# A two-layer graph attention, feed-forward and expert kernel: weight making moved to the first stage, rows written twice, rows in place

## The chip, the cores and the metric

The kernel runs on one core of a Trainium2 chip. The metric is the device time of one execution in microseconds. The engines are PE (matrix products), DVE (vector), ACT (scalar, with function tables), POOL (GpSimd) and SP (which issues most of the DMAs). A DMA that is issued on an engine's queue waits there for its semaphores in order with that engine's other work; it "lands" when its completion is signalled.

## The reference

All sizes: 4096 nodes, 256 features, 4 heads of 64 features, an int32 adjacency of 4096 x 4096.

```python
# --- layer 0 (adj_ffn) ---
x = x + _L0_gnn_ref(_layernorm(x, axis=-1), adj, L0_gnn_W, L0_gnn_a1, L0_gnn_a2)
x = x + _L0_ffn_ref((_layernorm(x, axis=-1))[None], L0_ffn_ln_w, L0_ffn_ln_b, L0_ffn_W, L0_ffn_b)[0]
# --- layer 1 (adj_ffn) ---
x = x + _L1_gnn_ref(L1_gnn_t, _layernorm(x, axis=-1), adj, L1_gnn_W1, L1_gnn_a1, L1_gnn_W2, L1_gnn_a2)
x = x + _L1_ffn_ref((_layernorm(x, axis=-1))[None], ...)[0]
```

The graph attention takes h = x W for each head, f1 = h a1, f2 = h a2, a softmax over the neighbours of leaky_relu(f1_i + f2_j), its product with h, and elu. The second layer has two of them. The feed-forward of layer 0 repeats this step 30 times:

```python
h = h + 0.01 * jnp.tanh(h)
h = h * jax.nn.sigmoid(h)
h = _layernorm(h, ln_w, ln_b)
h = jnp.einsum('bsc,dc->bsd', h, W) + b
```

The feed-forward of layer 1 is a mixture of 6 experts with the best 2 of each row.

## The kernel before

The program has five stages, one after the other: the first attention (g0), the feed-forward, the two attentions of layer 1 (g1, g2), and the experts. A group is 4 tiles of 128 rows (512 rows); there are 8 groups.

**Attention.** Each attention first prepares: it loads the 8 groups, normalizes, transposes and multiplies them (`products`, L300), and in g0 turns the adjacency into a bit mask, a piece at a time. During this preparation the functions in `others` make weights: `late.pop` (L418) runs them at g = 0 and after g = 3 and g = 5, with `small_ps` as their one buffer in PSUM. Then comes the loop over 4 chunks of 1024 rows, 4 heads and 8 units each, 128 units in all. A unit makes signs (`step_of`: ACT L461, DVE L459), masks them on DVE (L567 above, L573 below) and multiplies on PE (L519). At a head's end ACT takes the lower sums out of PSUM (L468, `lo`), DVE adds the whole sums into the tile `u` (L472), and `close` finishes the head, one step in each of the next units: L482 to L494 on DVE, the exponential into the tile `e` (L497), then `finish` of `to_rows` (L622, L623), which writes the head's 64 columns of 1024 rows with a DMA on SP (L624). In g0 `begin` also loads the old rows x (L615) that are added. Tile `u` has one buffer, `e` one of its own.

**Feed-forward.** `slot(at)` is a software pipeline of 240 units (30 steps x 8 groups) that are `at`, `at-2`, `at-3` and so on. In the order of the engines' work: tanh on ACT (L826) and its addition on POOL (L827) for unit `at`; silu (L815), the half-precision upper and lower parts (L817 on ACT, L818 on DVE) and a transposing DMA on SP (L822) for `at-2`; transposes on PE (L796), their copy on ACT (L846), the reciprocal deviation (ACT L849, POOL L850 and L851) for `at-3`; products on PE (L863, L866) for `at-4`; and for `at-5` the result on DVE (L803), scaled and with the bias added, into `y`. The last step adds `last` in place of `bias`, and then POOL adds the attention's rows (L877), which SP had loaded again from `x1d` (L790), and SP writes the sum to `x2d` (L878). g1 takes the groups 0 to 3 straight from these tiles and loads the others.

Ahead of the loop stands its preparation (L699 to L774): groups 0 to 3 of `x1d` are loaded on POOL's queue, `measure` (DVE L676, L678), `rate` (ACT L684, POOL) and `init` (ACT L695) normalize the rows into `y`, and the layer norm's weight and the matrix are loaded on ACT's queue (L703 to L707), transposed, scaled, centred, and split into `wT` and `w16`. The first slots measure, rate and init the other groups.

The order of PE, DVE, ACT and POOL within the loops is that of the program text (`tc.manual_schedule`). Outside them, and for SP, a scheduler orders the work; it keeps each engine's queue in order. Loads of whole groups go through `load_ahead` (L92) into tiles named `rows` of a pool that is made after g0; in g0 that place holds adjacency pieces (`adj`).

In the last stage `numbers` makes integer ramps on POOL (L959 iota, L961 cast).

Of the kernel before, what the change touches and what calls it, by code (L numbers as in the profile page):

```python
# [23 lines left out]
P = 128  # L24
C = 256
# [21 lines left out]
def gnn_ffn_kernel(ctx: ExitStack, tc: tile.TileContext, a: dict, out: bass.AP):  # L47
# [19 lines left out]
    ones = const.tile([2 * H, P], F32, name="ones")  # L67
    nc.gpsimd.memset(ones, 1.0)
# [10 lines left out]
    x1d = dram.tile([N, C], F32, name="x1d")  # L79
    x2d = dram.tile([N, C], F32, name="x2d")  # L80
# [7 lines left out]
    stream = []  # L88

    def load_ahead(src, g, view=rows_of, queue=nc.sync):  # L90
        t = stream[-1].tile([P, G, C], F32, name="rows")
        queue.dma_start(t, view(src, g))  # L92
        ahead[g] = t
# [67 lines left out]
    def attention(tag, src, norm, w, others, chunks, first, ends, following):  # L161
# [7 lines left out]
        with ExitStack() as scope:  # L169
            lay = scope.enter_context(tc.tile_pool(name=f"{tag}_lay", bufs=1))  # L170
            vals = lay.tile([P, NT, H, 2, 2, DV], F16, name="vals")
            r = lay.tile([P, NT, H], F32, name="r")
            nf2 = lay.tile([P, NT, H], F32, name="nf2")
            hs = lay.tile([P, 1, H, DV], F32, name="hs")
            mask = [scope.enter_context(tc.tile_pool(name=f"{tag}_mask", bufs=4))]
# [20 lines left out]
            def load_piece(n):  # L196

                c, g, part = n // PER, n % PER // 4, n % 4
                i0 = c * CM * P + part * TR
                arow[n] = stream[-1].tile([P, 2, 8 * P], I32, name="adj")  # L200
                nc.sync.dma_start(
                    arow[n],
                    adj[i0 : i0 + TR, g * 8 * P : (g + 1) * 8 * P].rearrange("(p s) n -> p s n", s=2),
                )
# [28 lines left out]
            with ExitStack() as ps:  # L233
# [44 lines left out]
                def greatest():  # L278
# [8 lines left out]
                    nc.vector.tensor_scalar(dm, ident[: 2 * H, : 2 * H], fx, None, op0=OP.mult)  # L287
                    pt = small_ps()
                    nc.tensor.matmul(pt[:, : 2 * H], ones, dm, start=True, stop=True)
# [108 lines left out]
                for g in range(NG + 2):  # L398
# [19 lines left out]
                    if g in (3, 5) and late:  # L418
                        late.pop(0)()
# [56 lines left out]
            def close(c, h, u):  # L476
# [19 lines left out]
                e = end.tile([P, CM, D], F32, name="e")  # L496
# [40 lines left out]
            with tc.manual_schedule(engines={mybir.EngineType.DVE, mybir.EngineType.Activation}):  # L537
# [3 lines left out]
                for at in range(len(units) + LAG):  # L541
# [43 lines left out]
                    if first:  # L585
# [8 lines left out]
                        if at == len(units) - 30:  # L594
                            store_mask(len(chunks) * PER // 4 - 1)
                    if following and at == len(units) - 2 * following[0]:
                        for g in range(following[0]):
                            load_ahead(following[1], g, *following[2:])
# [7 lines left out]
    def to_rows(dst, src=None):  # L606
# [5 lines left out]
        def begin(t, n, h, work):  # L612
            if src is not None:
                old = work.tile([P, 8, D], F32, name="old")
# [3 lines left out]
        def finish(t, n, h, u, e, old):  # L618
# [5 lines left out]
            nc.sync.dma_start(block(dst, t, n, h), e)  # L624

# [9 lines left out]
    with tc.tile_pool(name="adj", bufs=2) as adjacency:  # L635
        stream.append(adjacency)
        attention("g0", x, True, w0, [make, *makers], [8, 8, 8, 8], True, to_rows(x1d, x), [])
    stream.append(ctx.enter_context(tc.tile_pool(name="stream", bufs=4)))

    with ExitStack() as scope:
        one = scope.enter_context(tc.tile_pool(name="f_one", bufs=1))
        wT = one.tile([P, C], F32, name="wT")  # L650
        w16 = one.tile([P, 2, C], F16, name="w16")
        scale = one.tile([P, 2], F32, name="scale")
        under = one.tile([P, 2, G], F32, name="under")
        eps = one.tile([P, 2], F32, name="eps")
        nc.gpsimd.memset(eps[:, :1], EPS)
        nc.gpsimd.memset(eps[:, 1:], EPS * 1e-4)
        bias = one.tile([P, C], F32, name="bias")
        last = one.tile([P, C], F32, name="last")
# [4 lines left out]
        x1 = {}  # L663

        def load(g, queue=nc.sync):
            if g not in ahead:
                load_ahead(x1d, g, queue=queue)
            x1[g] = ahead.pop(g)

        measured, rates = {}, {}  # L670

        def measure(g):
            st = small.tile([P, G, 6], F32, name="x_st")
            mv = measured[g] = small.tile([P, G, 2], F32, name="x_mv")
            for r in range(G):
                nc.vector.bn_stats(st[:, r, :], x1[g][:, r, :])  # L676
            for r in range(G):
                nc.vector.bn_aggr(mv[:, r, :], st[:, r, :])  # L678

        def rate(g):  # L680

            mv = measured.pop(g)
            rs = small.tile([P, G], F32, name="x_rs")
            nc.scalar.activation(rs, mv[:, :, 1], AF.Identity, scale=1e-4, bias=eps[:, 1:])  # L684
            nc.gpsimd.tensor_tensor(rs, rs, mhalf, OP.pow)
            nm = small.tile([P, G], F32, name="x_nm")
            nc.gpsimd.tensor_tensor(nm, mv[:, :, 0], rs, OP.mult)
            nc.gpsimd.tensor_scalar(nm, nm, -1.0, None, op0=OP.mult)
            rates[g] = rs, nm

        def init(g):
            t = x1.pop(g)
            rs, nm = rates.pop(g)
            for r in range(G):
                nc.scalar.activation(  # L695
                    y[:, g * G + r, :], t[:, r, :], AF.Identity, scale=rs[:, r : r + 1], bias=nm[:, r : r + 1]
                )

        for g in range(4):  # L699
            load(g, nc.gpsimd)  # L700
        with tc.tile_pool(name="f_prep", bufs=1) as prep, tc.tile_pool(name="f_pps", bufs=1, space=PSUM) as pps:
            ln = prep.tile([2 * KC, P], F32, name="ln")
            nc.scalar.dma_start(ln[:KC], a["L0_ffn_ln_w"].rearrange("(k p) -> k p", p=P))  # L703
            nc.scalar.dma_start(ln[KC:], a["L0_ffn_ln_b"].rearrange("(k p) -> k p", p=P))
            wr = prep.tile([P, KC, C], F32, name="wr")
            nc.scalar.dma_start(wr, a["L0_ffn_W"].rearrange("(k p) c -> p k c", p=P))
            nc.scalar.dma_start(bias, bcast_rows(a["L0_ffn_b"]))  # L707
            for g in range(3):
                measure(g)
                if g < 2:  # L710
                    rate(g)
            init(0)
            ps = pps.tile([P, 2 * KC], F32, name="ps_ln")
            nc.tensor.transpose(ps, ln, ident[: 2 * KC, : 2 * KC])
            lnT = prep.tile([P, 2 * KC], F32, name="lnT")
            nc.vector.tensor_scalar(lnT, ps, 100.0, None, op0=OP.mult)
            lbb = prep.tile([P, KC, P], F32, name="lbb")
            nc.vector.tensor_copy(lbb, lnT[:, KC:, None].to_broadcast([P, KC, P]))
            ps = pps.tile([P, KC, C], F32, name="ps_w")
            for k in range(KC):  # L720
                for o in range(KC):
                    nc.tensor.transpose(ps[:, k, o * P : (o + 1) * P], wr[:, o, k * P : (k + 1) * P], ident)
            raw = prep.tile([P, KC, C], F32, name="raw")
            nc.vector.tensor_copy(raw, ps)
            ps = pps.tile([P, C], F32, name="ps_b")
            for k in range(KC):
                nc.tensor.matmul(ps, lbb[:, k, :], raw[:, k, :], start=(k == 0), stop=(k == KC - 1))
            nc.vector.scalar_tensor_tensor(bias, bias, 100.0, ps, op0=OP.mult, op1=OP.add)

            nc.vector.tensor_scalar(last, bias, -100.0, 0.01, op0=OP.add, op1=OP.mult)  # L730
            for k in range(KC):
                nc.vector.tensor_scalar(raw[:, k, :], raw[:, k, :], lnT[:, k : k + 1], None, op0=OP.mult)
            ps = pps.tile([P, C], F32, name="ps_m")
            for k in range(KC):
                nc.tensor.matmul(ps, mean, raw[:, k, :], start=(k == 0), stop=(k == KC - 1))
            for k in range(KC):
                nc.vector.tensor_tensor(raw[:, k, :], raw[:, k, :], ps, OP.subtract)
            sq = prep.tile([P, KC, C], F32, name="sq")
            nc.vector.tensor_tensor(sq, raw, raw, OP.mult)
            ps = pps.tile([P, C], F32, name="ps_m")  # L740
            for k in range(KC):
                nc.tensor.matmul(ps, mean, sq[:, k, :], start=(k == 0), stop=(k == KC - 1))
            far = prep.tile([P, 4], F32, name="far")
            nc.vector.tensor_reduce(far[:, 0:1], ps, axis=AX.X, op=OP.max)
            nc.vector.tensor_scalar(far[:, 0:1], far[:, 0:1], TINY, None, op0=OP.add)
            nc.gpsimd.tensor_tensor(far[:, 1:2], far[:, 0:1], mhalf[:, :1], OP.pow)
            nc.vector.tensor_tensor(far[:, 1:2], far[:, 1:2], far[:, 0:1], OP.mult)
            nc.vector.tensor_reduce(far[:, 2:3], bias, axis=AX.X, op=OP.max, apply_absolute_value=True)
# [33 lines left out]
        def slot(at):  # L782
            if 0 < at and at + 3 < NG:
                load(at + 3)
# [595 lines left out]
```

## Time and profile before

| | us |
|---|---|
| median of 3 runs | 3007.22 (3007.0 to 3009.08) |
| profiled execution | 3008.46 |
| its span | 3006.8 |
| g0, preparation | 0 to about 94 |
| g0, loop and closing | 94 to 606 |
| feed-forward | 606 to about 1581 |
| g1, loop | 1648 to 2126 |
| g2, loop | 2205 to 2677 |
| experts | 2677 to 3007 |

The page gives the busy time of the engines over the span, and the costliest groups of instructions with their mean duration, the idle time before them and what ended most of it:

```profile
PE 2813.1 (94%) x33923; PEld 2568.3 (85%) x33923; DVE 2741.0 (91%) x5766; ACT 2462.0 (82%) x3132; POOL 1173.2 (39%) x1056
L461 ACT ACTIVATE st<-f1b,nf 128x1024 int8<-128x1024 f32 x1265 | 1334.2, 1142 | 29.9 <-PE acc L519 24.6
L827 POOL TENSOR_TENSOR th<-th,y 128x1024 f32<-128x1024 f32 x240 | 568.2, 2368 | 27.2 <-ACT th L826 4.4
L803 DVE SCALAR_TENSOR_TENSOR y<-po,z_rs,bias 128x256 f32<-128x256 f32 x928 | 384.4, 477 | 2.1 <-PE tp L796 0.7
L815 ACT ACTIVATE z<-th 128x1024 f32<-128x1024 f32 x240 | 251.2, 1047 | 8.6 <-POOL th L827 8.3
```

Read the last of these lines so: 240 silus on ACT took 251.2 us together, 1047 ns each, and ACT stood idle 8.6 us ahead of them, 8.3 of it until POOL's addition was done. Lines of the timeline, shown below, give the start, the busy time, the engine, the line, the operation and how many are merged; in brackets stands the idle time before it and what ended it. "SPq" is a DMA issue on SP.

### The profile page before, as it was taken

Reading aid. Unit: us, or ns where it says so; the run is one execution under the profiler, and the core shown is the slowest. Engines: PE = TensorE matmul, PEld = TensorE weight load, DVE = VectorE, ACT = ScalarE, POOL = GpSimd, SP = SyncE. Lnnn points to the kernel's source line nnn. Section 1 sums busy time; section 2 is a strip of 40 time slices with the busy share of each in tenths; the row PEclk is TensorE's granted clock in tenths of the full one; section 3 lists DMA queues with packets and bytes.
Section 4 is the critical chain, followed back from the end, with each engine's and each line's share of the span. In section 5 each row is a group of like instructions: output and inputs, shape, how many; then the busy total and the mean of one; then the engine's idle time right before and its main releaser. Section 6 shows DMA issues by size and latency. Waiting matters only on the chain. (4 is left out here: it accounts for less than half of the span.)

```text
span 3006.8 us, 82646 instructions
## 1 busy us (share of the span) xinstructions
PE 2813.1 (94%) x33923; PEld 2568.3 (85%) x33923; DVE 2741.0 (91%) x5766; ACT 2462.0 (82%) x3132; POOL 1173.2 (39%) x1056
## 2 busy tenths in 40 slices
PE   6899999979999999999998999999889999986996
PEld 5799999958888888888876999999789999975996
DVE  8999999989999999999998899999689999986775
ACT  5799999788888888888866999999699999963442
POOL 2000000089999999999993000000200000013663
PEclk9999999989999999999999999999999999997998
DMA  9999784143333333333343031220303132133253
GB/s 292 267 256 249 224 247 118 33 133 70 68 68 67 68 70 69 68 68 68 68 95 121 20 103 51 76 79 27 107 20 93 51 107 79 51 96 123 82 172 134
DMA packets 482899, 320.08 MB, mean 106 GB/s; under 512 B 416573, under 2 KB 443354, under 8 KB 476378
## 3 DMA queue, kind: packets, MB, share of 16 engines
q1 hardware_dynamic: 467698, 287.13, 35.6%
q0 software_dynamic: 7680, 21.51, 2.3%
q10 hardware_dynamic: 7144, 6.16, 0.6%
q8 instruction: 268, 4.39, 0.6%
q14 instruction: 109, 0.89, 0.1%
HBM read 183.00 MB, written 52.04 MB: 78 GB/s over the span
## 5 line engine op out<-in xcount | busy, mean ns | idle before, releaser
L519 PE MATMUL acc<-vals,st 128*128 128x130 f16 x12288 | 1431.1, 218 | 36.1 <-DVE u L472 27.9
L519 PE MATMUL acc<-vals,below 128*128 128x130 f16 x12288 | 1430.7, 221 | 12.6 <-DVE below L573 11.9
L461 ACT ACTIVATE st<-f1b,nf 128x1024 int8<-128x1024 f32 x1265 | 1334.2, 1142 | 29.9 <-PE acc L519 24.6
L519 PEld LDWEIGHTS <-below 128*128 128x128 fp8e4 x12288 | 1175.7, 96 | 49.4 <-issue 44.5
L519 PEld LDWEIGHTS <-st 128*128 128x128 fp8e4 x12288 | 1207.5, 98 | 9.6 <-DVE st L567 7.5
L863 PE MATMUL po<-wT,zT 128*128 128x256 f32 x1920 | 576.1, 382 | 7.4 <-ACT zT L846 7.4
L827 POOL TENSOR_TENSOR th<-th,y 128x1024 f32<-128x1024 f32 x240 | 568.2, 2368 | 27.2 <-ACT th L826 4.4
L866 PE MATMUL po<-w,zT 128*128 128x256 f16 x3840 | 577.9, 273 | 0.3 <-DMA zT<-z 0.3
L866 PEld LDWEIGHTS <-zT 128*128 128x128 f16 x3840 | 376.3, 98 | 161.6 <-DMA zT<-z 1.2
L573 DVE TENSOR_TENSOR below<-m,st 128x1024 int32<-128x1024 int32 x384 | 470.0, 1224 | 32.8 <-DVE st L567 1.3
L567 DVE TENSOR_TENSOR st<-st,m 128x1024 int32<-128x1024 int32 x384 | 467.5, 1217 | 0.2
L803 DVE SCALAR_TENSOR_TENSOR y<-po,z_rs,bias 128x256 f32<-128x256 f32 x928 | 384.4, 477 | 2.1 <-PE tp L796 0.7
L839 DVE BATCH_NORM_STATS2 z_st<-z 128x6 f32<-128x256 f32 x960 | 335.8, 413 | 0.0
L863 PEld LDWEIGHTS po<-wT,zT 128*128 128x128 f32 x1920 | 291.1, 192 | 17.4 <-ACT zT L846 9.0
L105 POOL TENSOR_TENSOR ln_rstd<-ln_rstd,mhalf 128x4 f32<-128x4 f32 x24 | 32.3, 1345 | 586.5 <-ACT acc L1033 491.8
L815 ACT ACTIVATE z<-th 128x1024 f32<-128x1024 f32 x240 | 251.2, 1047 | 8.6 <-POOL th L827 8.3
L826 ACT ACTIVATE th<-y 128x1024 f32<-128x1024 f32 x240 | 249.8, 1041 | 0.1
L850 POOL TENSOR_TENSOR z_rs<-z_rs,mhalf 128x4 f32<-128x4 f32 x240 | 245.7, 1024 | 0.0
L846 ACT COPY zT<-tp 128x512 f32<-128x512 f32 x240 | 140.4, 585 | 110.5 <-PE tp L796 110.4
L459 DVE TENSOR_SCALAR st<-f1b,nf 128x1024 int8<-128x1024 f32 x271 | 201.2, 743 | 8.4 <-PE acc L519 8.4
L436 POOL MEMSET hs<- 128x4 f32 x3 | 0.3, 101 | 491.9 <-DVE u L489 491.9
L818 DVE SCALAR_TENSOR_TENSOR z<-z,scale,z 128x512 f16<-128x512 f32 x240 | 179.4, 747 | 4.9 <-ACT z L817 4.9
(252 smaller groups left out, 2970.2 us busy)
## 6 DMA issues: line engine op xcount, KB each, us to landing
adj<-in_adj_dram SPq DMA_DIRECT2D x64, 1024.0 KB
m<-edges SPq DMA_DIRECT2D x32, 1024.0 KB
f1b<-fd SPq DMA_DIRECT2D x48, 512.0 KB
edges<-m SPq DMA_DIRECT2D x16, 1024.0 KB
y<-yd SPq DMA_DIRECT2D x16, 512.0 KB
ew<-in_L_ffn_expert_w_dram SPq DMA_DIRECT2D x18, 256.0 KB
t<-in_x_dram SPq DMA_DIRECT2D x8, 512.0 KB
old<-in_x_dram SPq DMA_DIRECT2D x16, 256.0 KB
```

The source lines that it names most:

```text
L461: nc.scalar.activation(out, f1, AF.Sign, bias=f2, scale=-1.0)
L519: nc.tensor.matmul(acc[:, i, cols], masked[part][:, at_i // TR, s, rows], v[:, cols], start=(j == 0 and part == 0), stop=(j == NT - 1 and ...
L567: nc.vector.tensor_tensor(above, above, whole, OP.bitwise_and)
L573: nc.vector.tensor_tensor(below, whole, above, OP.bitwise_xor)
L803: nc.vector.scalar_tensor_tensor(y[:, g * G + r, :], po[:, r, :], rstd[:, r : r + 1], last if end else bias, op0=OP.mult, op1=OP.add,)
L815: nc.scalar.activation(z, th.pop(u), AF.Silu, scale=0.01)
L826: nc.scalar.activation(th[at], y[:, g * G : (g + 1) * G, :], AF.Tanh, scale=0.01)
L827: ins = nc.gpsimd.tensor_tensor(th[at], th[at], y[:, g * G : (g + 1) * G, :], OP.add)
L839: nc.vector.bn_stats(st[:, r, :], z[:, r, :])
L850: nc.gpsimd.tensor_tensor(rs[u], rs[u], mhalf, OP.pow)
L863: nc.tensor.matmul(po[:, r, :], src[:, r * P : (r + 1) * P], wT, start=True, stop=False)
L866: nc.tensor.matmul(po[:, r, :], src16[:, part * G + r, :], w16[:, other, :], start=False, stop=(part == 1 and other == 1),)
```

## The change

1. The feed-forward's weight making becomes `load_ffn` and `make_ffn`, a fourth entry of `others` in g0's preparation, run after g = 6. Some of its operations change engine: the copy out of PSUM, two scalings, the square and the upper half of `w16` go to ACT, `last`, a product and the two of `under` to POOL.
2. `to_rows` gets a `twin`: each head of g0 is written to `x1d` and once more to `x1e`.
3. In all three attentions `e` is no longer a tile: the exponential goes into the second half of `u`, and the DMA writes from there. `old` shares the buffers of `lo`.
4. `add_last` adds `last` to a group of `x1e` by an accumulating DMA on POOL's queue: groups 0 to 5 in g0's last chunk, groups 6 and 7 in the feed-forward's slots 32 and 64.
5. A table `side` calls into g0's last units: loads of the groups 0 to 3 at 28 units before the end, measures, rates, and the first two inits, which now work in place. Groups 4 to 7 go to a pool `hold`. In the first step tanh and the addition read these tiles, not `y`. After the first step each tile is loaded with its rows of `x1e`.
6. In the last step the result (L803 before) is added in place into that tile, and SP writes it to `x2d` at once; L877 and `last` as an operand are gone.
7. `ring`, one tile of 4 groups, takes the place of both pools, for the adjacency pieces and the rows; `ones` is gone (a factor C and `mean` instead); `numbers` makes long ramps in four parts.

The core of the diff (of `make_ffn` only what differs from L699 to L774 beside names):

```diff
-                e = end.tile([P, CM, D], F32, name="e")
+                e = u[:, :, 1, :D]
                 nc.scalar.activation(e[:, :nt], o[:, :nt], AF.Exp)
...
+                    if len(units) - at in side:
+                        side[len(units) - at]()
...
-                    if g in (3, 5) and late:
+                    if g in (3, 5, 6) and late:
                         late.pop(0)()
...
-                old = work.tile([P, 8, D], F32, name="old")
+                old = work.tile([P, 4, 2, DV], F32, name="old", tag="lo", bufs=2)
+                old = old.rearrange("p i b c -> p (i b c)")[:, : 8 * D].rearrange("p (i d) -> p i d", d=D)
                 nc.sync.dma_start(old[:, :n], block(src, t, n, h))
...
             nc.sync.dma_start(block(dst, t, n, h), e)
+            if twin is not None:
+                nc.sync.dma_start(block(twin, t, n, h), e)
...
+    def load_ffn(prep):
+        ln = w16[: 2 * KC, 0, :].bitcast(F32)
+        nc.scalar.dma_start(ln[:KC], a["L0_ffn_ln_w"].rearrange("(k p) -> k p", p=P))
+        nc.scalar.dma_start(ln[KC:], a["L0_ffn_ln_b"].rearrange("(k p) -> k p", p=P))
+        wr = wT, last
+        for k in range(KC):
+            nc.scalar.dma_start(wr[k], a["L0_ffn_W"][k * P : (k + 1) * P, :])
+        nc.scalar.dma_start(bias, bcast_rows(a["L0_ffn_b"]))
+        return ln, wr
...
+        nc.scalar.copy(raw, ps)
...
+        nc.gpsimd.tensor_scalar(last, bias, -100.0, 0.01, op0=OP.add, op1=OP.mult)
+        for k in range(KC):
+            nc.scalar.activation(raw[:, k, :], raw[:, k, :], AF.Copy, scale=lnT[:, k : k + 1])
...
+        nc.scalar.activation(sq, raw, AF.Square)
...
+        nc.gpsimd.tensor_tensor(far[:, 1:2], far[:, 1:2], far[:, 0:1], OP.mult)
...
+        nc.scalar.activation(w16[:, 0, :], raw[:, 1, :], AF.Copy, scale=scale[:, 1:])
...
+    def init(g):
+        rs, nm = rates.pop(g)
+        for r in range(G):
+            nc.scalar.activation(
+                x1[g][:, r, :], x1[g][:, r, :], AF.Identity, scale=rs[:, r : r + 1], bias=nm[:, r : r + 1]
+            )
+
+    def add_last(g):
+        nc.gpsimd.dma_start(rows_of(x1e, g), last[:, None, :].to_broadcast([P, G, C]), accum_op=OP.add)
...
+    side = {
+        28: [(load, g) for g in range(4)],
+        **{24 - 3 * g: [(add_last, g)] for g in range(6)},
+        14: [(measure, 0)],
+        8: [(measure, 1)],
+        4: [(rate, 0), (rate, 1), (measure, 2)],
+        1: [(measure, 3), (init, 0), (init, 1), (rate, 2), (rate, 3)],
+    }
+    attention(
+        "g0",
+        x,
+        True,
+        w0,
+        [make, *makers, (load_ffn, make_ffn)],
+        [8, 8, 8, 8],
+        True,
+        to_rows(x1d, x, x1e),
+        [],
+        {k: functools.partial(many, *v) for k, v in side.items()},
+    )
...
-            if 0 < at and at + 3 < NG:
-                load(at + 3)
             g = at - (units - NG - 4)
             if 0 <= g < NG // 2:
-                load(g)
+                load_ahead(x1e, g)
+                x1[g] = ahead.pop(g)
             elif NG // 2 <= g < NG:
-                x1[g] = work.tile([P, G, C], F32, name="x1", bufs=NG - NG // 2)
-                nc.sync.dma_start(x1[g], rows_of(x1d, g))
+                load_apart(x1e, g)
...
+                t = x1.pop(g) if end else None
                 for r in range(G):
                     nc.vector.scalar_tensor_tensor(
-                        y[:, g * G + r, :],
+                        t[:, r, :] if end else y[:, g * G + r, :],
                         po[:, r, :],
                         rstd[:, r : r + 1],
-                        last if end else bias,
+                        t[:, r, :] if end else bias,
                         op0=OP.mult,
                         op1=OP.add,
                     )
+                if end:
+                    nc.sync.dma_start(rows_of(x2d, g), t)
+                    if g < NG // 2:
+                        ahead[g] = t
...
-                nc.scalar.activation(th[at], y[:, g * G : (g + 1) * G, :], AF.Tanh, scale=0.01)
-                ins = nc.gpsimd.tensor_tensor(th[at], th[at], y[:, g * G : (g + 1) * G, :], OP.add)
+                was = x1.pop(at) if at < NG else y[:, g * G : (g + 1) * G, :]
+                nc.scalar.activation(th[at], was, AF.Tanh, scale=0.01)
+                ins = nc.gpsimd.tensor_tensor(th[at], th[at], was, OP.add)
...
-            if at + 2 < NG:
-                rate(at + 2)
-            if at + 1 < NG:
-                init(at + 1)
-            if at + 3 < NG:
-                measure(at + 3)
+            if 4 <= at + 3 < NG:
+                rate(at + 3)
+            if 2 <= at + 2 < NG:
+                init(at + 2)
+            if 4 <= at + 4 < NG:
+                measure(at + 4)
+            if at in (4 * NG, 8 * NG):
+                add_last(NG - 3 + at // (4 * NG))
...
-            u = at - 5
-            if units - NG <= u < units:
-                g = u % NG
-                t = x1.pop(g)
-                nc.gpsimd.tensor_tensor(t, t, y[:, g * G : (g + 1) * G, :], OP.add)
-                nc.sync.dma_start(rows_of(x2d, g), t)
-                if g < NG // 2:
-                    ahead[g] = t
```

## The prediction

> **What bounds the kernel now.** I read the page first (span 3006.8 us; PE busy 94%, DVE 91%, ACT 82%), then the busy time of each engine stage by stage, then the timeline around the feed-forward's two ends, then the timeline of the row writes. Columns of the first view: stretch, length, busy time of PE, weight loads, DVE, ACT, POOL, granted clock, DMA share, GB/s.
>
> ```profile
> 50.00:94.00 44.00, 29.29 (x126) 22.54 (x125) 41.91 (x77) 34.02 (x52) 15.98 (x24) 0.94 0.98 299
> 344.00:470.00 126.00, 119.78 (x2051) 118.28 (x2049) 122.64 (x130) 126.00 (x129) 0.00 (x0) 1.00 0.83 238
> 666.00:1545.00 879.00, 879.00 (x6280) 719.79 (x6279) 876.88 (x2915) 762.86 (x1122) 841.86 (x675) 1.00 0.35 68
> 1648.00:2120.00 472.00, 466.08 (x7996) 464.27 (x7997) 436.97 (x486) 437.05 (x441) 0.00 (x0) 0.99 0.18 57
> ```
>
> The second half of the first attention's preparation is bound by DVE (41.91 of 44.00). Its loop is bound by ACT (126.00 of 126.00) with DVE close behind. The feed-forward loop is bound by PE and DVE together; nothing in it is removed except at its ends. The second attention is PE's. So a gain can come only from the feed-forward's ends, and a loss from whatever lands on DVE or PE in the attentions.
>
> The start of the feed-forward, on DVE and ACT:
>
> ```profile
> 598.83 1.45 DVE L472 TENSOR_TENSOR u<-acc,lo 128x520 f32<-128x520 f32 x2
> ...
> 609.80 2.82 DVE L739 TENSOR_TENSOR sq<-raw 128x512 f32<-128x512 f32 x1
> 616.10 2.29 DVE L747 TENSOR_TENSOR far<-far 128x1 f32<-128x1 f32 x1 [0.70 <-POOL far L746]
> 621.74 0.72 DVE L818 SCALAR_TENSOR_TENSOR z<-z,scale,z 128x512 f16<-128x512 f32 x1
> 596.56 0.60 ACT L468 ACTIVATE lo<-acc 128x520 f32<-128x520 f32 x1 [8.64 <-PE acc L519]
> 620.44 0.72 ACT L817 ACTIVATE z<-z,scale 128x512 f16<-128x512 f32 x1 [1.86 <-DVE inv L763]
> ```
>
> The last head's closing starts at 598.83, and the weight's scale is ready only at 620.4, which ACT waits for. The end of the feed-forward:
>
> ```profile
> 1559.33 2.37 POOL L877 TENSOR_TENSOR rows<-rows,y 128x1024 f32<-128x1024 f32 x1
> 1561.65 2.80 POOL L827 TENSOR_TENSOR th<-th,y 128x1024 f32<-128x1024 f32 x1
> 1564.49 1.06 ACT L815 ACTIVATE z<-th 128x1024 f32<-128x1024 f32 x1 [4.44 <-POOL th L827]
> 1566.07 0.78 PE L863 MATMUL po<-wT,zT 128*128 128x256 f32 x2 [2.59 <-ACT zT L846]
> 1587.27 1.40 DVE L100 BATCH_NORM_STATS2 ln_st<-rows 128x6 f32<-128x256 f32 x4 [3.10 <-DMA rows<-x2d]
> ```
>
> The last additions (L877) stand on POOL ahead of the tanh additions (L827); ACT and then PE wait, and later DVE waits for a row load that stood on SP behind the writes of L877. Last, the row writes, which the change makes others wait for (SP and DVE):
>
> ```profile
> 1766.62 0.37 SPq L624 DMA_DIRECT2D h1d<-e  x1
> 1770.45 0.70 DVE L472 TENSOR_TENSOR u<-acc,lo 128x520 f32<-128x520 f32 x1 [0.74 <-ACT lo L468]
> 1796.62 0.37 SPq L624 DMA_DIRECT2D h1d<-e  x1
> 1799.22 0.92 SPq L92 DMA_DIRECT2D rows<-h1d  x2
> 1800.41 0.70 DVE L472 TENSOR_TENSOR u<-acc,lo 128x520 f32<-128x520 f32 x1
> PE acc L519 <- DVE u L472: 27.9, 45, 3.0
> ```
>
> A write issued at 1796.62 had landed by 1799.22, for then SP was let go to read it (2.6 us); the next use of u on DVE came 3.8 us after the issue. The last line (who waited for whom: total, times, longest) says that at nearly every head PE already waits for that DVE addition, so a delay there passes on to PE.
>
> **What the Trainium skill says.** "DMA: Bandwidth & Descriptors", section "Anatomy of one DMA — SWDGE (gpsimd) path", fits a DMA at about 2.0 us plus its bytes over 436 GB/s; for 256 KB that is 2.6 us, as the write at 1796.62 took, and for 512 KB 3.2 us, where the trace shows 6.0 us for POOL's row loads in the first attention, so I use the trace. The same page's "SWDGE vs HWDGE vs iDMA" gives accumulation during a transfer to GpSimd alone, so POOL issues the new ones; no such transfer is in the trace. Its "Rules for kernel authors" say that an accumulate beside another access of the same bytes must be waited for: hence the waits on SP below. "SBUF — State Buffer", "Who interferes with whom", says that a DVE instruction with two SBUF inputs contends with GpSimd's reads; L747, one element per partition, took 2.29 us beside 0.15 us for L750 of the same size, which agrees.
>
> **The change part by part.**
>
> *Weight making leaves the start.* Between 606.4 (last write issued) and 621.7 DVE has L728 to L772 in its way. In the changed kernel ACT's queue reads: both lower sums, tanh of 0, init 2, tanh of 1, the exponential of the last closing, init 3, table load, first z. The exponential needs DVE's closing chain, which starts no earlier than about 598.4 (measures 3, 4 and 5 at 1.75 each from 593.2) and takes 1.45 + 3 x 0.70 + 0.20 + 0.67 = 4.4 to it: 603. Then 0.63 + 2.06 + 1.28 + 1.05 + 0.72 puts the first low part of z16 (L818 before, L852 after) at about 610 instead of 621.74: 11.7 us. Slots with an init take 5.47 us (621.74 to 647.70 has five), those without 3.8; one init fewer stands in the slots, 1.7 more. Groups 6 and 7 still wait for the last row write (4.7 us from issue to landing at 606.39, now with a second write behind it) and may give a microsecond back. I take -13 (-10 to -14.5). Late next is ACT with its remaining inits.
>
> *That work in the first preparation.* DVE gets lnT 0.15, bias 0.42, two subtractions 0.75, two reductions 0.83, some nine small ones 1.3, wT 0.38 and w16 0.45: 4.3 us, where it is busy 41.91 of 44.00. PE's transposes and six products go through one small PSUM buffer, six more turns between PE and an evacuating engine; five more DMAs stand on ACT's queue ahead of its first computation at 15.43 (0.4 to 1.6 each for such issues there), with some 2.8 us until xT of the first group would be missed (the first weights are ready at 19.5). ACT and POOL have room. I take +5 (+2 to +10).
>
> *Rows written twice.* 16 more writes of 256 KB in 256-byte pieces, about 1.1 us of all 16 engines each (share 0.44 + 0.71 in the two microseconds of the write at 1797), per head of 31 us at a share of 0.83 to 0.91. Nothing in the first loop waits for DMA but 2.6 us once. Zero by itself; what it costs if the cover goes is the 4 heads of the first chunk times 1.1.
>
> *Rows in place: e becomes a part of u.* The additions into u (L472) now wait for the landing of the last head's writes; queued behind them on DVE are the mask operations, and PE waits for both. From write issue to next L472 the first loop has 3.5 to 5.95 us, seven of eleven intervals at 4.15 or more; the pair should land after 3.5 to 5. Stall 0 to 1 us on most, of which DVE's idle 0.8 us per head hides some: +5 (0 to +18). In the second and third attention (3.5 to 4.5 us for 2.6 to 3.2) there is room, except where 1 MB of mask is loaded just ahead: there DMA was busy until 1771.1, and L472 came at 1770.45. Six such heads, 0.5 to 1.5 with the chain behind: +3 (0 to +7).
>
> *Measures, init and rate at the end of the first loop.* Three measures (5.2 us) go into a chunk where DVE has 119.98 of 126.00 busy; inits fall into ACT's 8.64 idle. +1 (0 to +2).
>
> *Accumulating DMAs.* Six are in the first loop, with POOL idle. Two are in the feed-forward (slots 32 and 64): 0.75 to 1.2 us of issue on POOL, and on SP the load of that group stands ahead of a transposing DMA (L822) whose result PE takes about 2.3 us after it lands now. With 6.0 us to landing, much of it spent before that load's turn comes, this is just covered, with 10 it costs 4 each. Page and trace bound it at 3.2 and, doubled for reading and writing, 12. I take +1 (0 to +6).
>
> *The last step.* Eight L877 (2.35 each) go from POOL. Slots 238 and 239 took 6.3 us instead of 3.92: 4.8; PE's stop of 2.59 was followed by matmuls of 1.06 instead of 0.60 at a granted clock near 0.5, partly inside that. PE should end about 1574 instead of 1579.3: -5.3. The write no longer waits for POOL, so the load of group 4 goes out early and the 3.10 at 1587 goes: -2.7 more. DVE's own last row (PE to L803 to write) is late next. -8 (-5.5 to -9).
>
> *Integer ramps in four pieces.* In the last stage ln_rstd (L105) stands behind 4.3 instead of 6.7 us of POOL work, and DVE idled 2.4 there: -1.5 (-2 to 0).
>
> Sum: -13 -8 -1.5 +5 +5 +3 +1 +1 = -7.5. The profiled execution took 3008.46, its span 3006.8; the span after is then 2999.3, the execution about 3001. The median of the runs, 3007.22, is 1.2 below the profiled one, so 2999.7: **3000**.
>
> **Rivals.** (1) *The waits for landing decide* (the other side). Place: L472 at every head. 16 us of gain are left after the preparation and small costs of 7, so from a mean stall of 16 / 45 = 0.36 us per head the change doesn't pay. If the double write lands 2 us late in the first loop's heads (12 x 2 = 24) and the others lose 0.5 (33 x 0.5 = 16), it is 40 instead of 8: about 3032. For it: DMA share near 1 there and allowances of 3.5. Against: 2.6 measured in the quiet stages. (2) *Costs hidden*: preparation +2, waits +2, the gains whole at -22.5: 3007 - 18 = 2989. For it: DVE's spare time and PE's waits that are there already. (3) *The preparation eats the start*: one small buffer and late first ACT work cost 12 instead of 5: 3007. For it: DVE at 41.91 of 44; against: POOL and ACT are half idle. (4) The accumulates block SP: +6 more, inside the ranges.
>
> **How the numbers follow.** Forecast (2993 to 3006) 0.42; waits decide (3013 to 3045) 0.27; costs hidden (2984 to 2993) 0.18; preparation eats it (3001 to 3013) 0.13. A measurement of this kernel tells 0.2%, 6 us, from no change: below 3001.2 lie the hidden costs and most of the forecast (0.18 + 0.31), within lie the rest of it and the third rival (0.11 + 0.13), above lies the first. Range: 2986 to 3026, which leaves out a little below and about half of the first rival. The forecast's own is 2993 to 3006.
>
> **What would show it.** Right: the first L852 near 610 plus the preparation's and loop's delays; no idle above 1 us on ACT before the last tanh sums; the loop of the first attention beginning at 99 instead of 94. Wrong: DVE idle "<-DMA" at L472's successor above 10 us in sum, PE waits for it well above 27.9; idle on PE for zT in slots 32 and 64; the first attention's preparation longer by 10.

## The result, and the profile after

The changed kernel takes 3014.05 us (median of 18 runs, 3008.73 to 3017.73), the kernel before 3007.49 on the same chips; the ratio is 1.0021, 95% interval 1.0014 to 1.0028: 6 us slower, where 7 us faster was forecast. The profiled spans are 3013.7 and 3006.8.

The same DVE operations can be found in both traces (the addition into u, L472 before and L475 after; the lower part of z16, L818 and L852), and the difference of their start times is a lag that can be followed through the program:

| lag of the changed kernel at | us | step | forecast |
|---|---|---|---|
| first addition into u (g0's preparation and its first head) | 5.6 | +5.6 | +5 |
| first addition into u of g0's last head | 20.0 | +14.3 | +6 |
| feed-forward, slot 12 | 10.2 | -9.8 | -13 |
| feed-forward, slots 71 to 236 | 17.3 | +7.1 | +1 |
| first addition into u of g1 | 6.4 | -10.9 | -8 |
| last addition into u of g2 | 10.2 | +3.8 | +3 |
| end of the span | 6.9 | -3.3 | -1.5 |

All signs are as forecast. The gains are 24.0 us in sum (22.5 forecast); the losses are 30.8 instead of 15. The difference came mostly in the first loop and in the slots 32 and 64.

First, who waited for whom in the changed kernel (total us, times, longest). The first two lines are of the whole program, the third of g0's loop alone:

```profile
PE acc L522 <- DVE u L475: 37.3, 45, 3.2
DVE u L475 <- DMA h1d<-u: 11.3, 4, 5.5
DVE u L475 <- DMA x1e<-u: 6.9, 8, 1.8
```

The new waits for landing are there: with g2's, DVE's idle time for them is 22.2 us in 15 places. PE's wait for that addition went from 27.9 to 37.3. (The 5.5 in the second line is the closing of g1's last head, where DVE stood 4.5 us for ACT's lower sums before, too.)

The timeline of g0's fifth head and the one after it, on POOL, SP and DVE:

```profile
266.76 2.93 POOL L766 DMA_DIRECT2D x1e<-last  x2 [167.48 <-DMA x1e<-u]
271.03 6.40 SPq L220 DMA_TRANSPOSE m<-pair  x1
288.49 1.23 DVE L217 TENSOR_SCALAR pair<-ring 128x2048 int8<-128x2048 int32 x1 [2.62 <-DMA ring<-in_adj_dram]
301.91 0.70 DVE L475 TENSOR_TENSOR u<-acc,lo 128x520 f32<-128x520 f32 x1 [1.68 <-DMA x1e<-u]
```

Two accumulating DMAs start at 266.8, two more at 397.4, and only the last two in the last chunk, at 524.1: POOL has nothing else to do in this loop, and its queue waits only for a chunk's writes to land. DMA is full at 266.8. A transposing DMA of the mask then takes 6.40 us to issue (at most 2.97 in g0's loop before), and DVE stands for an adjacency piece and for a landing. This head is 4.5 us longer. The slow issue alone does not explain it: behind the pair at 397.4 a transposing DMA takes 7.07 us, but DVE doesn't stand for a piece there, and that head is 0.2 longer.

Slot 32 of the feed-forward, on POOL, SP and PE:

```profile
759.81 1.37 POOL L766 DMA_DIRECT2D x1e<-last  x1
767.57 1.47 POOL L885 TENSOR_TENSOR z_rs<-z_rs,mhalf 128x4 f32<-128x4 f32 x1
782.76 1.02 POOL L885 TENSOR_TENSOR z_rs<-z_rs,mhalf 128x4 f32<-128x4 f32 x1
766.79 0.36 SPq L802 DMA_DIRECT2D x<-x1e  x1
772.97 0.61 PE L903 MATMUL po<-w,zT 128*128 128x256 f16 x4 [3.09 <-DMA zT<-z]
774.42 1.06 PE L900 MATMUL po<-wT,zT 128*128 128x256 f32 x2
```

The accumulating DMA is issued at 759.8; SP's load of that group, which waits for it, goes at 766.8, so it took 7.0 us to land. The transposes behind it on SP come late, PE stands 3.09 us, and then its matmuls take 1.06 instead of 0.60 for some 3 us. The lag grows by 4.9 here. At slot 64 the same wait is 1.88 us, the matmuls keep their 0.60, and the lag grows by 2.0. Remember POOL's power (the operation that makes the reciprocal deviation, L850 before, L885 after), with 1.47 just behind slot 32 and 1.02 once PE had stood: it matters below.

The feed-forward's start, on DVE:

```profile
620.09 2.55 DVE L485 TENSOR_TENSOR u<-u,r 128x520 f32<-128x520 f32 x1
622.68 2.85 DVE L489 TENSOR_TENSOR u<-u 128x520 f32<-128x520 f32 x1
633.03 0.75 DVE L852 SCALAR_TENSOR_TENSOR z<-z,scale,z 128x512 f16<-128x512 f32 x1 [3.66 <-ACT z L851]
```

The weight making is gone, but two additions of the closing take 2.55 and 2.85 instead of 0.70. At the other end the DVE line that waited 3.10 us for its rows now waits 0.57:

```profile
1595.87 1.41 DVE L101 BATCH_NORM_STATS2 ln_st<-ring 128x6 f32<-128x256 f32 x4 [0.57 <-DMA ring<-x2d]
```

### The profile page after: what moved, and what is told of

The parts are those of the page before. It is cut to its first block, busy times and chain, and to the rows that moved or that the text cites. A ratio compares the mean times of both kernels' runs of the same rounds, so it can differ in the third digit from the quotient of the medians.

```text
span 3013.7 us, 82658 instructions
## 1 busy us (share of the span) xinstructions
PE 2807.6 (93%) x33923; PEld 2568.8 (85%) x33923; DVE 2736.0 (91%) x5756; ACT 2465.6 (82%) x3137; POOL 1168.4 (39%) x1061
## 5 line engine op out<-in xcount | busy, mean ns | idle before, releaser
L522 PE MATMUL acc<-vals,st 128*128 128x130 f16 x12288 | 1437.5, 219 | 48.9 <-DVE u L475 37.3
L862 POOL TENSOR_TENSOR th<-th,y 128x1024 f32<-128x1024 f32 x232 | 549.9, 2370 | 23.6 <-DVE z L852 4.4
L900 PEld LDWEIGHTS po<-wT,zT 128*128 128x128 f32 x1920 | 291.1, 192 | 11.7 <-ACT zT L881 3.4
L885 POOL TENSOR_TENSOR z_rs<-z_rs,mhalf 128x4 f32<-128x4 f32 x240 | 248.7, 1036 | 3.1 <-ACT z_rs L884 3.1
L861 ACT ACTIVATE th<-y 128x1024 f32<-128x1024 f32 x232 | 241.7, 1042 | 0.0
L852 DVE SCALAR_TENSOR_TENSOR z<-z,scale,z 128x512 f16<-128x512 f32 x240 | 179.9, 750 | 8.2 <-ACT z L851 8.1
```

The costliest lines, as they stand in the source:

```text
L522: nc.tensor.matmul(acc[:, i, cols], masked[part][:, at_i // TR, s, rows], v[:, cols], start=(j == 0 and part == 0), stop=(j == NT - 1 and ...
L861: nc.scalar.activation(th[at], was, AF.Tanh, scale=0.01)
L862: ins = nc.gpsimd.tensor_tensor(th[at], th[at], was, OP.add)
L885: nc.gpsimd.tensor_tensor(rs[u], rs[u], mhalf, OP.pow)
L900: nc.tensor.matmul(po[:, r, :], src[:, r * P : (r + 1) * P], wT, start=True, stop=False)
```

## The experiments

Every ratio is to the kernel before on the same chip, with a 95% interval. "Loop" is the growth of the lag from the first to the last head of g0 (additions into u, first of each head), 14.3 in the changed kernel.

**The exponential in u alone.** The kernel before, with `e = u[:, :, 1, :D]`.

> The kernel before with one edit: the exponential goes into the second half of u and the row write starts there; one write for each head, nothing else. Theory A (the waits of the additions into u for the landing of a row write cost what the traces show): g1 and g2 lose 3 to 4 us at the heads with a mask load just ahead, g0 loses 2 to 4, together +5 to +8 us. Rival B (those stalls only move a wait that PE had anyway): under 2 us.

Measured: 1.0041 (1.0027 to 1.0055), 12 us slower, nearly twice what was expected in the middle. In the trace g0's additions waited 6.1 us for landings (9 times), its loop is 5.5 longer, and g1 and g2 lost 4.7. So theory A is right in kind, and its numbers were too small; one small edit that frees a tile costs about half of the 24.0 us that the whole change gains.

**Two writes alone.** The kernel before, with the second DMA in `finish`.

```diff
             nc.sync.dma_start(block(dst, t, n, h), e)
+            if twin is not None:
+                nc.sync.dma_start(block(twin, t, n, h), e)
```

> The kernel before with each head of g0 written twice from the tile e, which nothing reads afterwards; no wait is added for DVE. If the bytes alone cost the first loop its time (DMA share near 1), the loop of g0 gets 4 to 10 us longer and the transposing DMAs of the mask take longer to issue on SP; if only the wait for the second landing costs, it is within 1 us of before.

Measured: 1.0006 (0.9997 to 1.0015), loop +1.9, of which 0.3 in the first three chunks, where the mask is made and DMA is full. The bytes alone cost nothing that can be told from zero.

**The early accumulations held back.** The changed kernel; in `add_last`, for g < 6 (shortened):

```diff
+            tc.add_manual_dep(ins.ins, masked_last[0].ins.name, ..., reason="not before this unit")
```

> The changed kernel with the six accumulating DMAs of g0 held back to the units of the last chunk by a dependency on a mask operation there. Theory: in the changed kernel they start as soon as a chunk's writes have landed, two at 266.8 us, where the DMA engines are full, and cost the head after it 3 to 4 us: the time falls by 3 to 5 us. Rival: their transfers fit in, and the long head is that of the double writes: within 1 us of the changed kernel.

Measured: 1.0013 (1.0003 to 1.0023) where the changed kernel has 1.0021: 2 us, less than expected and with intervals that overlap. In the trace the head in question is 0.7 longer instead of 4.5, the next one 1.7 instead of 0.6, and the loop is 11.7. In the other runs that issue them at the same point this head is 2.0 to 4.5 longer when the additions into u wait for landing, and 0.7 when they don't (the run without waits, below): the accumulations cost mostly through these waits.

**SP freed in the slots 32 and 64.** The changed kernel; the loads of groups 6 and 7 depend on a late operation of the loop:

```diff
-                load_apart(x1e, g)
+                load_apart(x1e, g, lowers[-1] if g >= 6 else None)
```

> The changed kernel with the loads of the groups 6 and 7 of x1e held back to the feed-forward's last step, so that SP does not wait for the accumulating DMAs of the slots 32 and 64 ahead of the loop's transposing DMAs. Theory (SP is blocked): the lag of 4.9 and 2.0 us at these slots goes, -6 to -7 us, and no PE idle for zT is left there. Rival (the issue on POOL and its port cost them): -1 us or less.

Measured: 1.0072 (1.0056 to 1.0089), 21 us slower than before. Both numbers failed. As the theory said, PE doesn't stand for `zT` in these slots any more, and the lag at slot 36 is smaller (7.4); but from there it grows by 0.1 us in every slot, 22 us to the loop's end. The rival named the issue on POOL, which the next two runs bear out, but expected no gain and no loss. Who waited for whom, and POOL's and DVE's timeline in the middle of the feed-forward:

```profile
ACT z L857 <- POOL th L871: 127.6, 209, 1.9
1206.06 2.36 POOL L871 TENSOR_TENSOR th<-th,y 128x1024 f32<-128x1024 f32 x1
1208.39 1.46 POOL L894 TENSOR_TENSOR z_rs<-z_rs,mhalf 128x4 f32<-128x4 f32 x1
1209.93 0.20 POOL L895 TENSOR_TENSOR z_rs<-z_rs,under 128x4 f32<-128x4 f32 x1
1208.01 0.96 DVE L860 SCALAR_TENSOR_TENSOR z<-z,scale,z 128x512 f16<-128x512 f32 x1
```

The same three in the kernel before, in a slot of 3.92 us:

```profile
1002.73 1.02 POOL L850 TENSOR_TENSOR z_rs<-z_rs,mhalf 128x4 f32<-128x4 f32 x1
1003.83 0.42 POOL L851 TENSOR_TENSOR z_rs<-z_rs,under 128x4 f32<-128x4 f32 x1
1003.44 0.74 DVE L818 SCALAR_TENSOR_TENSOR z<-z,scale,z 128x512 f16<-128x512 f32 x1
```

POOL's three operations follow each other without a gap: 2.36 + 1.46 + 0.20 = 4.02 us per slot, where PE's slot is 3.92 and POOL had 2.36 + 1.02 + 0.42 = 3.80 before. In the kernel before, the power runs mostly beside the results that DVE reads out of PSUM (L803), and the multiplication behind it beside DVE's lower part; now the power starts beside the lower part (0.96 instead of 0.74). That this is what makes it longer is read from what stands beside it in nearly all slots of both kinds; no run separates it. ACT waits for POOL in nearly every slot. In the changed kernel, while PE stood and DVE with it, POOL caught up and then stood itself (3.56 us for DVE at 780.4), and the power went back to 1.02. The block of SP cost 7 us there and, by the 22 of this run, saved some 15 (an estimate from these two runs).

**A bump on POOL, without any DMA.** The kernel before; in slot 32 only:

```diff
+                if at == 4 * NG:
+                    nc.gpsimd.tensor_tensor(junk, y[:, :2, :], y[:, 2:4, :], OP.add)
```

> The kernel before with one more addition on POOL in the feed-forward's slot 32 (128 x 512, about 1.2 us; nothing reads its result) and no other edit, no DMA. Theory (the feed-forward's loop has two steady states, and a delay on POOL of over a microsecond takes it from 3.92 us per slot to about 4.02, where POOL's square root stands beside a DVE operation on the shared port and takes 1.47 instead of 1.02): from slot 35 on the lag grows by about 0.1 us per slot to the end, +15 to +21 us in all. Rival (the loop catches up with such a delay, and the slow state needs a DMA or a late load): +2 us or less.

```profile
751.13 1.27 POOL L854 TENSOR_TENSOR junk<-y 128x512 f32<-128x512 f32 x1
754.68 1.46 POOL L851 TENSOR_TENSOR z_rs<-z_rs,mhalf 128x4 f32<-128x4 f32 x1
```

Measured: 1.0067 (1.0048 to 1.0086), 20 us slower for one operation of 1.27 us. The lag is 1.7 at slot 30, 4.7 at slot 62 and 22.8 at slot 235. As expected, then: the loop of the kernel before has two steady states, and once it is in the slower one, where POOL has no gap, it doesn't leave it in the 200 slots that follow. The profile before had the sign already: in the loop's last step, where L877 delays POOL, two powers took 1.46 (the first at 1557.6).

**No accumulation in the loop.** The changed kernel; groups 6 and 7 loaded late, and POOL adds the constant:

```diff
-            if at in (4 * NG, 8 * NG):
-                add_last(NG - 3 + at // (4 * NG))
+            if units <= at < units + 2:
+                t = x1[at - units + 6]
+                nc.gpsimd.tensor_tensor(t, t, last[:, None, :].to_broadcast([P, G, C]), OP.add)
```

> The changed kernel without accumulating DMAs in the feed-forward's loop: the groups 6 and 7 are loaded late and POOL adds the constant after the loop. Theory (the issue on POOL puts its square root beside a DVE operation that uses the same port, a state of 4.02 us per slot that stays until PE stops; the block of SP ended it in the changed kernel): no lag at the slots 32 and 64, all slots at 3.92, the time falls by 7 us. Rival (the late loads of groups 6 and 7 bring the slow state themselves, since they were in the run free_sp too): slots at 4.02 again, 10 us or more slower than the changed kernel.

Measured: 1.0006 (0.9997 to 1.0014), 4 to 5 us below the changed kernel's 1.0021. The lag stays at 10.0 from slot 30 to slot 235, so all 7.1 us of the loop are gone, and late loads are harmless. (The scheduler put the two additions into the last slots, where the lag grows by 3 us.)

**The waits for landing taken away.** The changed kernel, both writes kept:

```diff
-                e = u[:, :, 1, :D]
+                e = u[:, :, 1, :D] if first else end.tile([P, CM, D], F32, name="e")
...
-            nc.vector.scalar_tensor_tensor(e, e, 1.0, u, op0=OP.min, op1=OP.add)
+            out = e if old is None or dst is x3d else old
+            nc.vector.scalar_tensor_tensor(out, e, 1.0, u, op0=OP.min, op1=OP.add)
+            e = out
```

In g0 the tile `old` takes its turn with `lo`, so ACT's second lower sum may wait for a landing, later than the addition did. (The expectation names g2 beside g0; in the kernel that ran, g2 writes from the exponential's own tile, as g1 does.)

> The changed kernel with the waits for landing moved away from the additions into u, both writes kept: in g0 and g2 the last operation of a head puts its result into the tile old, from where it is written, and in g1 the exponential has a tile of its own. Theory A (those waits are most of the 14.3 us that the first loop lost and all that g1 and g2 lost): the loop of g0 gets 6 to 9 us shorter than in the changed kernel, g1 and g2 together 3 to 4, the time falls by 8 to 12. Rival (the bytes of the second write and the accumulations cost the loop its time): g0 keeps its loss, and the time falls by 3 to 4.

Measured: 1.0002 (0.9994 to 1.0011), 5 to 6 us below the changed kernel. The loop is 8.7 instead of 14.3; from g1's first to g2's last addition the lag grows by 1.0 instead of 3.8. Theory A holds in kind, with 5.6 and 2.8 where it said 6 to 9 and 3 to 4. Of the 5.6, 3.7 are in the one head beside the accumulating DMAs.

**The weights loaded later.** The changed kernel; the five DMAs of `load_ffn` depend on a later copy of `xT`.

> The changed kernel with the five DMAs of the feed-forward's weights on ACT's queue held back until a third group's transposes are copied. Theory (they delay ACT's first copy, which came at 22.2 us instead of 16.7, and the preparation never wins that back): the first addition into u comes 4 to 5 us earlier and the time falls by as much. Rival (DVE's added 4.3 us in its full half are the cause): 1 us or less.

Measured: 1.0027 (1.0017 to 1.0037). ACT's first copy came at 16.9 us, as before the change (16.7), and not at 22.2; the first addition into u still came 5.5 late. So ACT's late copy is not what makes that addition late. Whether it is DVE's 4.3 us or the turns through one PSUM buffer wasn't separated.

**The closing not disturbed.** The changed kernel; POOL's additions of slots 0 and 1 depend on the closing's multiplication (L497).

> The changed kernel with POOL's first two additions of the feed-forward held behind the multiplication that ends the last head's closing. Theory (these additions, which now stand beside the closing, stretch its two additions on DVE from 0.70 to 2.55 and 2.85 us, and so the exponential and the first silu come 4 us late): the two take 0.70 again and the feed-forward's slot 12 comes 3 to 4 us earlier after the end of g0. Rival (what the closing gains, the later additions lose again): 1 us or less.

The operation that took 2.55, and who waited longest on DVE in the first slots:

```profile
619.32 0.70 DVE L486 TENSOR_TENSOR u<-u,r 128x520 f32<-128x520 f32 x1
DVE x_st L746 <- DMA x<-x1d: 6.8, 1, 6.8
```

Measured: 1.0026 (1.0016 to 1.0037). The closing takes 0.70 for each again, and slot 2 comes 10.2 after the last head's first addition into u instead of 14.2. But the measure of group 6 stands behind it on DVE and waits 6.8 us for the group's load, which waits for the last row write; slot 7 comes 1.3 later than in the changed kernel. So the rival holds for the time, and the theory for the two long additions.

**All of it together, three times.** One write to `x1d`, to which the constant is accumulated for groups 0 to 3 in the last chunk, after they are loaded; POOL adds it for groups 4 to 7; no wait at the additions into u; weights loaded later.

> All of it together, and no second copy: the rows are written once to x1d, the constant is accumulated there for the groups 0 to 3 after they have been loaded, in the last chunk, and POOL adds it for the groups 4 to 7 after the loop; no wait for landing at the additions into u; weights loaded after the first groups. From the traces: 6.9 us over before, less 4 (loads), less 8 to 12 (waits), less 7 (loop), less 1 to 2 (bytes): 13 to 18 us faster than before, near 2992.

Measured: 1.0076 (1.0063 to 1.009). The scheduler put POOL's four additions into the slots up to 10. The lag grows by 8.5 us from slot 5 to slot 10, and the loop stays in its slower steady state for the 230 slots that follow. g0's loop is 5.8, g1 and g2 lose nothing.

> The run best with two dependencies more: POOL's additions of the constant stand behind the loop's last addition, so that nothing disturbs POOL in the loop, and the first two additions of the feed-forward stand behind the closing. Expected from the other runs: the preparation +3 to +6, the loop of g0 +6, the start of the feed-forward -13, no lag in the loop, its end -10, g1 and g2 0, the experts 0 to -3: 11 to 16 us faster than before, about 2994.

Measured: 0.9967 (0.9955 to 0.9979), 10 us faster than before; this chip took 3024.12 for the kernel before. The loop of the feed-forward keeps its lag (4.1 from slot 30 to 235).

> The run best2 with the measures, rates and inits of the groups 6 and 7 one slot later. In best2 DVE stood 5.9 us at the measure of group 6 for that group's load, which waits for the last row write. Theory (that wait holds up the lower part of the next slot, so it is what is late next after the closing): slot 3 comes 4 to 5 us earlier and the time is 3 to 5 us below best2, about 0.9955 of before. Rival (the init that now stands a slot later costs as much): the same as best2, 0.9967.

Measured: 0.9963 (0.995 to 0.9977), 2996.64 where the kernel before takes 3006.87. Slot 3 comes 4.4 us earlier after the closing's multiplication, slot 11 2.7 us, as the theory said; between this run and the one before it the intervals tell nothing apart. Both are faster than both kernels.

## Why the prediction was wrong

The gains came as forecast in sum. Two terms of the losses failed: the accumulating DMAs in the feed-forward's loop, and those in g0's loop, which had no price.

- **The accumulations in the feed-forward's loop** (+1, "0 to +6") measured 7.1, and all of it goes when they go. This is the step whose failure is shown most clearly. SP's block was named as the way, with 6.0 us to landing as just covered; it was 7.0, and PE's stop with slower matmuls behind it made 4.9 at slot 32. What was not thought of is POOL's side: its issue was counted (0.75 to 1.2 us), but no price was put on the delay, and a delay of over a microsecond tips the loop into its slower state. In this change the block hid that; without it the same edit costs 22 us.
- **The six accumulations in g0** were priced at nothing, "with POOL idle". They were also misplaced: I took the units of the call for the time of the issue, but the program text gives each engine its order, not its time, and an idle POOL runs ahead to the first moment its semaphores allow, where DMA is full. Together with the waits the head behind the first pair lost 2.0 to 4.5; holding all six back shortened the loop by 2.7, and the time by no more than the noise.
- **The waits for landing** in g0 (+5) measured 5.5 in the run with the exponential in u alone, and 5.6 by taking them away, where 3.7 are shared with the accumulations; in g1 and g2 (+3) the same two runs give 4.7 and 2.8. Mechanism and place were right, and the sizes lie in the ranges, though the time of the small edit alone (12 us) is more than these sums. The landings with a mask load ahead are the ones seen in g1 (2.50, 2.01 and 1.29 of DVE idle) and g2 (1.77, 1.36 and 0.87), for an expected 0.5 to 1.5 each. Rival 1 put them at up to 40, which they weren't; the total came out on its side by the sum of other terms, so its number was luck.
- **The end of g0's loop** (+1): the head with the first two measures is 2.8 longer, and 2.8 to 3.5 in every version of the changed kernel. DVE's idle was counted over the chunk (6 us in 126); where these two stand, 3.5 us together, it was 1.7 before. Another 1.5 us come at the last chunk's first head. Their cause is open: most runs have them, with one write and with two.
- **The feed-forward's start** (-13): 9.8. POOL's additions now stand beside the closing. The Trainium skill, "SBUF — State Buffer", section "Who interferes with whom", has the rule, that a DVE instruction with two SBUF inputs contends with GpSimd's reads, and I quoted it for the operations that leave (L747), but didn't ask what the moved ones now stand beside. 0.70 became 2.55 and 2.85. But this is not the whole: held apart alone it brought nothing, since the load of group 6 is late next. With both taken away, in the last run, the start gains 11.8.
- **The feed-forward's end** (-8): 10.9, by the mechanism that was forecast. **The preparation** (+5): 5.6, though not by ACT's late copy; in all versions of the changed kernel it lay between 3.4 and 7.2. **The integer ramps** (-1.5): the wait that was named fell from 2.38 to 0.60 (0.6 to 0.9 in the other versions of the changed kernel), and the operation behind it comes about 2.0 us sooner after the last addition into u in all of them. How much of the stage's 3.3 that is stays open, since it also gained 2.8 in the run with two writes alone, which doesn't touch it.

Of the 14.4 us between the forecast span and the measured one, 8.3 are g0's loop, 6.1 the slots 32 and 64, 3.2 the start; end, g1, g2, preparation and last stage give 3.3 back.

Most of the signs of being wrong came: DVE idle for landings above 10 us in sum (22.2), PE's wait well above 27.9 (37.3), PE idle for `zT` in both slots (3.09 and 1.88). The 22.2 us of idle cost far less than that: PE's wait for this addition grew by only 9.4 us, and DVE's wait for ACT's lower sums at the same place fell from 48.3 to 37.1.

Four readings of the prediction were off, none of them decisive. The five slots with an init take 5.2 us each on average (25.96 in all), not 5.47. The steps to the first lower part add up to 608.7, which was put down as 610. Of the first loop's intervals between a write and the next addition there are fifteen, nine of them at 4.15 or more. And the fit for DMAs issued on POOL was set beside a write on SP's queue, whose 2.6 us is an upper bound.

## What to carry to other kernels

An engine that is busy 96% of a loop's period, as POOL was here, need not be one with 4% of slack: ask what a single delay of a microsecond does to its phase, and whether the neighbour that it then stands beside makes it slower than the bound; adding one operation in one slot is a cheap way to find out. When work is moved, price what it stands beside at the new place, and find out where each queue really issues it, since an idle queue runs ahead of the place in the program text. And a tile that is saved by writing a DMA from the accumulator of the next round puts what the landing takes beyond the gap onto the engine chain; that small edit alone cost 12 us.

## What the runs showed of the hardware that was not expected

- One addition of 1.27 us on POOL in slot 32 of 240 cost 20 us. POOL's power of 128x4 elements takes 1.02 us beside DVE's results out of PSUM and 1.46 where it starts beside one DVE operation of two SBUF inputs, the multiplication behind it 0.20 instead of 0.42, and the period became 4.02 instead of 3.92.
- Two accumulating DMAs of 512 KB, issued back to back while the DMA engines were full, took 16.6 us to land (median of the two); one in the quiet feed-forward took 7.0. The Trainium skill, "DMA: Bandwidth & Descriptors", section "Anatomy of one DMA — SWDGE (gpsimd) path", gives by its fit 3.2 us for 512 KB; no run here shows a plain one of that size on POOL's queue under 5.3 (four were issued in a row).
- While the two ran, the issue of a transposing DMA on SP took 5.6 and 6.4 us instead of the usual 1.3.
